# Four graph layers on one core: float32r parts for every source tile of the second layer, evacuation straight out of PSUM, and another split of the first layer's piece buffers

## The chip, the core and the metric

The kernel runs on one core of a Trainium2 chip. A core has a matrix engine (TensorE, in the profile PE, with its weight loads as PEld), VectorE (DVE), ScalarE (ACT), GpSimd (POOL) and SyncE (SP), which here mostly issues transfers. Each engine works through its own list of instructions. The metric is the device time of one execution in microseconds, given as the median of several runs.

## The reference

There are 3327 nodes with 512 features, and one adjacency matrix for all layers. Layers 0 to 2 are graph attention layers with 8, 4 and 8 heads, each behind a layer norm with ReLU and with a residual:

```
h = relu(layernorm(x));  Wh = h @ W, split by heads
e[i, j] = leaky_relu(s1[i] + s2[j], 0.2)     where adj[i, j] > 0, else minus infinity
x = x + elu(softmax_j(e) @ Wh)
```

s1 and s2 are products of Wh with two vectors per head. Layer 1 (the second layer) also sets the diagonal of its mask, and its four heads have 128 features each. Layer 3 averages the neighbours' features, joins them with the node's own, and applies dense weights.

## The kernel before, in words

**The arithmetic.** exp(leaky_relu(s1 + s2)) is exp(s1) exp(s2) where s1 + s2 is positive, and the same with 0.2 times each where it is not. So a head needs no exponent per edge: for each sign there is a 0/1-like matrix (mask and sign, in fp8), multiplied with Wh scaled by exp(s2) or exp(0.2 s2). A column of ones gives the softmax's denominator, so a head of layer 1 has DA = 129 columns. The two results of a target row are scaled by a coefficient of that row (L.c, made by `close_terms`, L561 to L599, from all s1 and s2), added, and divided by the denominator.

**Tiles and groups.** Targets and sources lie in 26 tiles of 128 nodes. Target tiles are taken in chunks of four (the last has two); source tiles come in five groups of 6, 6, 6, 4 and 4 (JG, L67). For each chunk and head, ScalarE or VectorE compares s1 with -s2 for every source tile (L660 to L665; the list GP_ON_DVE names VectorE's tiles), VectorE combines it with the mask (`split`, L668), and TensorE accumulates over the 26 source tiles for two target tiles at a time: one "pass".

**Precision.** The scaled Wh is kept in parts, so that cheap matmuls add up to enough bits. Layers 0 and 2 use three bf16 pieces side by side. In layer 1 the kind of a group (KIND, L49) says how: "b" is three bf16 pieces, 387 columns, multiplied with the fp8 matrix as it is (L756); "s" and "v" are two float32r parts, 258 columns (L753), for which the fp8 matrix must first be cast to float32r by ScalarE ("s", tile ts, three buffers) or by VectorE ("v", tile tv, two buffers), in `real`, L628 to L634. A cast covers one group and the two target tiles of one pass. Before, the kinds are b, s, s, v, v. The parts are made while the previous layer runs (`pieces`, L363; `parts`, L449) and stored to device memory; each head loads them again (L708, tile ab).

**Layer 1, one head.** Two signs times two passes. The matrices of the positive sign are used first; then VectorE flips them in place to the other sign (L788). After each pass VectorE sums the three 129-column pieces of each accumulator into R (L774; the third holds only what group 0 put there). At the head's end R is multiplied by L.c (L796), the signs are added (L798), and the rows are divided into A (L800 to L803). There are four accumulators of one PSUM bank each.

**Layer 0.** Its pieces come in two rings: groups of six tiles in "ab" with 7 buffers, groups of four, once the first pass is over, in "abx" with 3 (`pieces_tile`, L639). All are loaded over SP's queue (L714), where transposing transfers of the adjacency (tile tr, L238, three buffers), mask stores (L252) and the rows of s1 (L676) are issued too.

**Order.** The program's text gives priorities; a planner of the framework then fixes each engine's order when the kernel is built, and an instruction whose inputs and buffer are ready earlier can stand ahead of one written before it. `after` adds orders by hand. Small stages of the next layer (layer norm, transposes, projections) are started once per pass by `hooks.run` (L608, L784).

Of the kernel before, what the change touches and what calls it, by code (L numbers as in the profile page):

```python
# [25 lines left out]
F32 = mybir.dt.float32  # L26
BF16 = mybir.dt.bfloat16
# [10 lines left out]
P = 128  # L38
# [4 lines left out]
S2_MAX = 30.0  # L43
S_CLIP = 40.0

GP_ON_DVE = [(5, 12, 19), tuple(range(18, 26)), (4, 9, 14, 19, 24)]


KIND = "bssvv"  # L49


@with_exitstack
def tile_gnn(ctx: ExitStack, tc: tile.TileContext, x, adj, W0, a01, W1, al, ar, W2, a2,
# [60 lines left out]
    for l in range(3):  # L114
        H, DA, AO, HW = dims(l)
        if l == 1:
            abd.append([dram.tile([H, 2, P, nj, AO], BF16, name=f"ab{l}_{g}") if KIND[g] == "b" else
                        dram.tile([H, 2, P, nj, 2 * DA], F32, name=f"ab{l}_{g}") for g, (_, nj) in enumerate(JG)])
# [92 lines left out]
    def mask_steps(pool, t, g):  # L211


        n = pn(t)
        c, k = where[t]
        j0, nj = JG[g]
        w = min(nj * P, N - j0 * P)
        q = {}

        def load():  # L220
            at = q["at"] = pool.tile([P, JM * P], BF16, name="at", bufs=3)
            if n < P:
                nc.vector.memset(at, 0.0)
            elif w < nj * P:
                nc.vector.memset(at[:, w:nj * P], 0.0)
            ld = nc.gpsimd.dma_start(at[:n, :w], adj[t * P:t * P + n, j0 * P:j0 * P + w])
            after(ld, gone[-1] if gone else stored[NT - 1] if c else relus[-3])

        def turn():
            at = q["at"]  # L230
            if c == 0:
                tp = q["tp"] = ps.tile([P, 8, P], BF16, name="tp", bufs=2)
                for j in range(nj):
                    nc.tensor.transpose(tp[:, j, :], at[:, j * P:(j + 1) * P], identb)
                compare()
            else:
                tp = q["tp"] = mp.tile([P, JM, P], BF16, name="tr", bufs=3)
                tr = nc.sync.dma_start(tp[:, :nj], at[:, :nj * P], transpose=True)  # L238
                after(tr, gone[-1] if gone else stored[NT - 1])

        def compare():
            hooks.done += 1
            tp = q["tp"]
            st = masks0[g][:, k] if c == 0 else pool.tile([P, JM, P], FP8, name="st", bufs=3)[:, :nj]
            cm = nc.vector.tensor_scalar(st, tp[:, :nj], 0.0, 2.0, op0=ALU.is_gt, op1=ALU.mult, saturate=False)
            if gone:
# [116 lines left out]
    def pieces(L, t, AB, pool, first, behind=None):  # L363
# [4 lines left out]

        o, two = (t % 2, 2) if first else (0, 1)
        if o == 0:  # L370
            L.pt = pool.tile([P, H, 2, two, AO] if l == 1 else [P, H, two, HW], BF16, name="pt", bufs=3 if first else 2)
        pt = L.pt
        nc.gpsimd.memset(pt[:, :, :, o, 3 * DA:AO] if l == 1 else
                         pt[:, :, o].rearrange("p h (a w) -> p h a w", a=2)[..., 3 * DA:AO], 1.0)

        def dst(s, a):
            if l == 1:
                return pt[:, :, a, o, s * DA:(s + 1) * DA]
# [14 lines left out]
        if o == two - 1 and l == 1:  # L393
            for a in range(2):
                L.to_store.append((abd[l][g][:, a, :, js, :].rearrange("h p j w -> p h j w"), pt[:, :, a]))
        elif first and o == two - 1:
# [52 lines left out]
    def parts(L, t, AB, pool, first, behind=None):  # L449
# [229 lines left out]
    def attention(L, hooks, open_next, close):  # L679
# [5 lines left out]
        for c, (t0, nt) in enumerate(chunks):  # L685
# [3 lines left out]
            for h in range(H):  # L689
# [10 lines left out]
                for a in range(2 if l == 1 else 1):  # L700
                    row = []
                    for g, (_, nj) in enumerate(JG):
                        if l == 1:
                            tl = mp.tile([P, JM * 2 * DA], F32R, name="ab", bufs=7)
                            two = KIND[g] != "b"
                            w = 2 * DA if two else AO
                            v = (tl if two else tl.bitcast(BF16))[:, :nj * w].rearrange("p (j w) -> p j w", j=nj)
                            ld = nc.sync.dma_start(v.bitcast(F32) if two else v, abd[l][g][h, a])  # L708
# [28 lines left out]
                for a in range(2 if l == 1 else 1):  # L737
# [5 lines left out]
                    for ks, js in passes:  # L743
                        thr = {}
                        for j in js:
                            g, jj = jwhere[j]
                            if l == 1 and KIND[g] != "b" and g not in thr:
                                thr[g] = real(a, g, ks, th)
                            for k in ks:
                                if j == 0:  # L750
                                    acc[k] = accs.tile([P, 512], F32, name="acc")
                                if g in thr:
                                    mm = nc.tensor.matmul(acc[k][:, :2 * DA], thr[g][:, k - ks[0], jj, :], ab[a][g][:, jj, :],  # L753
                                                     start=(j == 0), stop=(j == NT - 1), skip_group_check=True)
                                elif l == 1:
                                    mm = nc.tensor.matmul(acc[k][:, :3 * DA], th[a][g][:, k, jj, :], ab[a][g][:, jj, :3 * DA],  # L756
                                                     start=(j == 0), stop=(j == NT - 1), skip_group_check=True)
                                else:
                                    o = 1 if deg else 0
# [9 lines left out]
                            load_y2(yp, 0, late)  # L769
                        if js[-1] != NT - 1:  # L770
                            continue
                        for k in ks:
                            if l == 1:
                                nc.vector.tensor_reduce(R[:, k, a, :], acc[k][:, :3 * DA].rearrange("p (s d) -> p d s", s=3),  # L774
                                                        AX.X, ALU.add)
# [20 lines left out]
                nc.vector.tensor_mul(Rv, Rv, L.c[:, t0:t0 + nt, :, h:h + 1].to_broadcast([P, nt, 2, DA]))  # L796
                num = R[:, :, 0, :]
                nc.vector.tensor_add(num[:, :nt], Rv[:, :, 0, :], Rv[:, :, 1, :])  # L798
                rc = mp.tile([P, PER, 1], F32, name="rc")
                nc.vector.tensor_scalar(rc[:, :nt], num[:, :nt, DK:DA], S_MIN, None, op0=ALU.max)  # L800
                nc.vector.reciprocal(rc[:, :nt], rc[:, :nt])
# [88 lines left out]
    lay_out(bp, ("ab", JM * 400, BF16, 7))  # L890
    ip = masking.enter_context(tc.tile_pool(name="masks", bufs=1))
    with tc.tile_pool(name="first", bufs=1) as fp:

# [50 lines left out]
    tags = [[A[0], R, tht, ("tr", JM * P, BF16, 3), ("abx", 4 * 400, BF16, 3), gt],  # L944
            [A[1], ("ab", JM * 258, F32R, 7), R, ("ts", 2 * JM * P, F32R, 3), ("tv", 2 * 4 * P, F32R, 2), tht[:3] + (10,)],
            [A[2], ab, ("R", PER * 2 * 65, F32, 1), tht, gt]]
    hooks.masks = in_steps([mask_steps(ip, t, g) for t, g in order[20:]])
    for l in range(3):
# [530 lines left out]
```

## Time and profile before

| what | value |
|---|---|
| median of 3 runs | 3587.35 us (3585.51 to 3601.4) |
| the profiled execution's own time | 3590.36 us |
| its span, first to last instruction | 3588.6 us |
| mean granted TensorE clock | 0.988 |
| busy: PE, PEld, DVE, ACT, POOL | 96%, 87%, 73%, 70%, 18% |
| attention of layer 0 / of layer 1, by the windows view | 202 to 1268 us / 1268 to 2113 us |
| HBM read and written | 663.59 MB, 129.64 MB |

A line of groups names the source line, the engine, the operation, output and input tiles with their shapes and the count; then busy us and the mean ns of one; then the idle time of the engine just ahead of these instructions, and what ended it. A line of the timeline gives start, length, engine, the group and how many were merged; in square brackets stands the idle time ahead of it. The windows view gives each engine's busy time within a stretch. Matmuls overlap, so their pace is read from starts, not from durations.

### The profile page before, as it was taken

The numbers are of one execution on the slowest core, as the hardware profiler recorded it, in microseconds if no ns is written. First come the engines' busy times: TensorE is split into PE (matmuls) and PEld (weight loads), VectorE is DVE, ScalarE is ACT, GpSimd is POOL, SyncE is SP. The second block draws the span as 40 slices with busy tenths as digits, with TensorE's granted clock in tenths as the row PEclk, the third lists the DMA queues.
The fourth block names the chain that finished last, engine by engine and source line by source line (L and its number), as shares of the span: only waits on it lengthen the run. The fifth ranks groups of instructions, "written<-read, shape, count | busy, mean of one in ns | idle before, by whom it ended". The sixth has DMA issues, their size and how long they took to land. (4 is left out here: it accounts for less than half of the span.)

```text
span 3588.6 us, 77637 instructions
## 1 busy us (share of the span) xinstructions
PE 3452.1 (96%) x30751; PEld 3112.2 (87%) x30751; DVE 2622.2 (73%) x5227; ACT 2507.9 (70%) x4113; POOL 632.5 (18%) x858
## 2 busy tenths in 40 slices
PE   7889999999999999999999989999999999999998
PEld 6788999999999878888888869989898989876887
DVE  8777878787887789888888868877676767672221
ACT  5767877877887888888798767766676667572111
POOL 6601222111110211233223230001010101020000
PEclk9999999999999999999999999999999999999999
DMA  7798999999966877777877876655555555576331
GB/s 216 235 239 222 237 249 233 258 236 242 262 217 207 283 277 262 282 258 273 283 256 266 307 280 212 195 174 178 176 195 176 173 178 184 166 264 257 122 99 60
DMA packets 398119, 797.72 MB, mean 222 GB/s; under 512 B 112969, under 2 KB 221844, under 8 KB 397104
## 3 DMA queue, kind: packets, MB, share of 16 engines
q1 hardware_dynamic: 363890, 723.14, 62.5%
q0 software_dynamic: 28128, 62.42, 7.5%
q10 hardware_dynamic: 5726, 7.08, 0.6%
q8 instruction: 245, 4.01, 0.5%
q14 instruction: 130, 1.06, 0.1%
HBM read 663.59 MB, written 129.64 MB: 221 GB/s over the span
## 5 line engine op out<-in xcount | busy, mean ns | idle before, releaser
L664 ACT ACTIVATE gt<-s1b,ks 128x512 fp8e4<-128x512 f32 (+1 forms) x2448 | 1448.0, 677 | 294.3 <-issue 160.1
L760 PE MATMUL acc<-ab,tht 128*128 128x195 bf16 (+1 forms) x9112 | 1558.0, 248 | 11.3 <-DVE tht L668 9.2
L763 PE MATMUL acc<-ab,gt 128*128 128x195 bf16 (+1 forms) x9112 | 1557.1, 248 | 5.7 <-DVE rc L800 3.3
L763 PEld LDWEIGHTS <-gt 128*128 128x128 fp8e4 x10744 | 1055.5, 98 | 64.3 <-issue 41.5
L760 PEld LDWEIGHTS <-tht 128*128 128x128 fp8e4 x10744 | 1055.2, 98 | 35.2 <-DVE tht L668 20.0
L668 DVE TENSOR_TENSOR tht<-gt,m 128x768 uint32<-128x768 uint32 (+3 forms) x557 | 449.8, 808 | 121.8 <-ACT gt L664 120.1
L670 DVE TENSOR_TENSOR gt<-tht,m 128x768 uint32<-128x768 uint32 (+3 forms) x557 | 450.1, 808 | 8.7
L633 ACT CAST ts<-tht 128x1536 fp32r<-128x1536 fp8e4 x208 | 300.0, 1470 | 59.0 <-PE acc L753 54.9
L753 PE MATMUL acc<-ab,ts 128*128 128x258 f32 x2496 | 335.0, 290 | 4.9 <-DMA ab<-ab 2.5
L753 PEld LDWEIGHTS acc<-ab,ts 128*128 128x128 f32 x2496 | 314.6, 191 | 14.4 <-issue 3.3
L661 DVE TENSOR_SCALAR gt<-s1b,ns 128x512 fp8e4<-128x512 f32 (+1 forms) x446 | 217.3, 492 | 133.6 <-PE acc L763 127.9
L1015 PE MATMUL acc<-y,mf 128*128 128x512 f32 x1352 | 309.9, 391 | 2.3 <-DVE mf L1010 2.3
L664 ACT ACTIVATE tht<-s1b,ks 128x512 fp8e4<-128x512 f32 (+1 forms) x504 | 308.3, 680 | 2.9 <-DMA s1b<-s 2.4
L763 PE MATMUL acc<-abx,gt 128*128 128x195 bf16 (+1 forms) x1632 | 288.7, 250 | 20.8 <-DVE rc L800 7.8
L760 PE MATMUL acc<-abx,tht 128*128 128x195 bf16 (+1 forms) x1632 | 289.5, 250 | 19.3 <-DMA abx<-ab 15.5
L1015 PEld LDWEIGHTS acc<-y,mf 128*128 128x128 f32 x1352 | 253.6, 188 | 58.5 <-DVE mf L1010 2.7
L863 POOL TENSOR_TENSOR xt<-xt,e 128x512 f32<-128x512 f32 x72 | 122.1, 1695 | 899.6 <-DVE e L862 586.4
L778 DVE TENSOR_REDUCE R<-acc 128x130 f32<-128x390 f32 x416 | 214.7, 556 | 77.5 <-PE acc L763 76.9
L756 PE MATMUL acc<-ab,tht 128*128 128x387 bf16 x1248 | 226.6, 330 | 9.0 <-DMA ab<-ab 5.4
L1012 ACT CAST mf<-m 128x768 fp32r<-128x768 fp8e4 (+1 forms) x78 | 59.1, 762 | 245.8 <-PE acc L1015 234.0
L753 PE MATMUL acc<-ab,tv 128*128 128x258 f32 x1664 | 219.3, 283 | 2.5 <-DVE tv L633 1.4
L753 PEld LDWEIGHTS acc<-ab,tv 128*128 128x128 f32 x1664 | 207.3, 189 | 4.7 <-DVE tv L633 2.5
(163 smaller groups left out, 3722.6 us busy)
## 6 DMA issues: line engine op xcount, KB each, us to landing
ab<-ab SPq DMA_DIRECT2D x333, 600.0 KB, 5.2
ab<-ab SPq DMA_DIRECT2D x112, 774.0 KB, 6.6
ab<-ab SPq DMA_DIRECT2D x112, 516.0 KB, 5.4
ab<-ab SPq DMA_DIRECT2D x112, 400.0 KB, 3.8
abx<-ab SPq DMA_DIRECT2D x110, 400.0 KB, 6.9
ab<-ab SPq DMA_DIRECT2D x56, 582.0 KB, 7.3
s1b<-s SPq DMA_DIRECT2D x120, 256.0 KB, 6.4
m<-mask SPq DMA_DIRECT2D x69, 384.0 KB, 4.1
```

Source lines behind the costliest of these rows:

```text
L633: (nc.scalar.copy if KIND[g] == "s" else nc.vector.tensor_copy)(t[:, :k1 - k0, :nj], th[a][g][:, k0:k1])
L661: nc.vector.tensor_scalar(gv[:, :, jj, :], s1v, L.ns2[:, j, h:h + 1], 2.0, op0=ALU.is_gt, op1=ALU.mult, saturate=False)
L664: nc.scalar.activation(gv[:, :, jj, :], s1v, AF.Relu, bias=L.ks2[:, j, h:h + 1], scale=BIG, saturate=False)
L668: nc.vector.tensor_tensor(pu, gu, mu, ALU.bitwise_and)
L670: nc.vector.tensor_tensor(gu, pu, mu, ALU.bitwise_xor)
L753: mm = nc.tensor.matmul(acc[k][:, :2 * DA], thr[g][:, k - ks[0], jj, :], ab[a][g][:, jj, :], start=(j == 0), stop=(j == NT - 1), skip_grou ...
L756: mm = nc.tensor.matmul(acc[k][:, :3 * DA], th[a][g][:, k, jj, :], ab[a][g][:, jj, :3 * DA], start=(j == 0), stop=(j == NT - 1), skip_grou ...
L760: nc.tensor.matmul(acc[k][:, :3 * DA + o], th[0][g][:, k, jj, :], ab[0][g][:, jj, :3 * DA + o], start=(j == 0), stop=False, skip_group_che ...
L763: mm = nc.tensor.matmul(acc[k][:, AO:AO + 3 * DA + o], th[1][g][:, k, jj, :], ab[0][g][:, jj, AO:AO + 3 * DA + o], start=False, stop=(j == ...
L778: nc.vector.tensor_reduce(R[:, k], v.rearrange("p a (s d) -> p a d s", s=3), AX.X, ALU.add)
L863: nc.gpsimd.tensor_add(xt, xt, e)
L1015: nc.tensor.matmul(acc[k], mf[:, jj, :], y2[g][:, jj, s, :], start=(j0 + jj == 0 and s == 0), stop=(j0 + jj == NT - 1 and s == 1))
```

## The change

- Group 0 of layer 1 becomes "v": the kinds are v, s, s, v, v. All five groups now use two float32r parts, so every accumulator of layer 1 is 258 columns wide, and the bf16 branches for layer 1 (storing, loading, multiplying) go. tv keeps two buffers, each now for up to six source tiles; tht, the ring of the fp8 matrices of layer 1, goes from 10 to 9 buffers.
- Evacuation in layer 1: instead of one three-piece reduction per accumulator and a scaling and an addition at the head's end, each of the two 129-column halves is multiplied by the row's coefficient straight out of PSUM and added onto R's first plane: four instructions per pass. The coefficients must then exist at the first evacuation, so `close_terms` is called there.
- VectorE's compares of layer 1 go from the eight tiles 18 to 25 to the six tiles 18, 19, 20, 22, 23, 24; 21 and 25 go to ScalarE.
- Layer 0: "ab" 7 to 6 buffers, "abx" 3 to 4, "tr" 3 to 4.

```
-GP_ON_DVE = [(5, 12, 19), tuple(range(18, 26)), (4, 9, 14, 19, 24)]
-KIND = "bssvv"
+GP_ON_DVE = [(5, 12, 19), (18, 19, 20, 22, 23, 24), (4, 9, 14, 19, 24)]
+KIND = "vssvv"
...
-                tp = q["tp"] = mp.tile([P, JM, P], BF16, name="tr", bufs=3)
+                tp = q["tp"] = mp.tile([P, JM, P], BF16, name="tr", bufs=4)
...
-        if l == 1 and KIND[g] != "b":
+        if l == 1:
...
-            tl = mp.tile([P, nj * HW], BF16, name="abx", bufs=3)
+            tl = mp.tile([P, nj * HW], BF16, name="abx", bufs=4)
...
-            tl = pool.tile([P, JM * HW], BF16, name="ab", bufs=7)
+            tl = pool.tile([P, JM * HW], BF16, name="ab", bufs=6 if L.l == 0 else 7)
...
-                        pt = mp.tile([P, PER * JM * P], FP8, name="tht", bufs=10 if l == 1 else 7)
+                        pt = mp.tile([P, PER * JM * P], FP8, name="tht", bufs=9 if l == 1 else 7)
...
-                            if l == 1 and KIND[g] != "b" and g not in thr:
+                            if l == 1 and g not in thr:
                                 thr[g] = real(a, g, ks, th)
...
-                                elif l == 1:
-                                    mm = nc.tensor.matmul(acc[k][:, :3 * DA], th[a][g][:, k, jj, :], ab[a][g][:, jj, :3 * DA],
-                                                     start=(j == 0), stop=(j == NT - 1), skip_group_check=True)
...
+                        if l == 1 and c == 0 and h == 0 and a == 0 and ks[0] == 0:
+                            close_terms(L)
                         for k in ks:
                             if l == 1:
-                                nc.vector.tensor_reduce(R[:, k, a, :], acc[k][:, :3 * DA].rearrange("p (s d) -> p d s", s=3),
-                                                        AX.X, ALU.add)
+                                cf = L.c[:, t0 + k, a, h:h + 1]
+                                for s in range(2):
+                                    v = acc[k][:, s * DA:(s + 1) * DA]
+                                    if a == s == 0:
+                                        nc.vector.tensor_scalar(R[:, k, 0, :], v, cf, None, op0=ALU.mult)
+                                    else:
+                                        nc.vector.scalar_tensor_tensor(R[:, k, 0, :], v, cf, R[:, k, 0, :],
+                                                                       op0=ALU.mult, op1=ALU.add)
...
-                if c == 0 and h == 0:
-                    close_terms(L)
-                Rv = R[:, :nt]
-                nc.vector.tensor_mul(Rv, Rv, L.c[:, t0:t0 + nt, :, h:h + 1].to_broadcast([P, nt, 2, DA]))
                 num = R[:, :, 0, :]
-                nc.vector.tensor_add(num[:, :nt], Rv[:, :, 0, :], Rv[:, :, 1, :])
+                if l != 1:
+                    if c == 0 and h == 0:
+                        close_terms(L)
+                    Rv = R[:, :nt]
+                    nc.vector.tensor_mul(Rv, Rv, L.c[:, t0:t0 + nt, :, h:h + 1].to_broadcast([P, nt, 2, DA]))
+                    nc.vector.tensor_add(num[:, :nt], Rv[:, :, 0, :], Rv[:, :, 1, :])
...
-            [A[1], ("ab", JM * 258, F32R, 7), R, ("ts", 2 * JM * P, F32R, 3), ("tv", 2 * 4 * P, F32R, 2), tht[:3] + (10,)],
+            [A[1], ("ab", JM * 258, F32R, 7), R, ("ts", 2 * JM * P, F32R, 3), ("tv", 2 * JM * P, F32R, 2), tht[:3] + (9,)],
```

More of the change, by code (lines that the diff above doesn't have):

```diff
@@ L116, in tile_gnn @@
         if l == 1:
-            abd.append([dram.tile([H, 2, P, nj, AO], BF16, name=f"ab{l}_{g}") if KIND[g] == "b" else
-                        dram.tile([H, 2, P, nj, 2 * DA], F32, name=f"ab{l}_{g}") for g, (_, nj) in enumerate(JG)])
+            abd.append([dram.tile([H, 2, P, nj, 2 * DA], F32, name=f"ab{l}_{g}") for g, (_, nj) in enumerate(JG)])
         else:
@@ L370, in pieces @@
         if o == 0:
-            L.pt = pool.tile([P, H, 2, two, AO] if l == 1 else [P, H, two, HW], BF16, name="pt", bufs=3 if first else 2)
+            L.pt = pool.tile([P, H, two, HW], BF16, name="pt", bufs=3 if first else 2)
         pt = L.pt
-        nc.gpsimd.memset(pt[:, :, :, o, 3 * DA:AO] if l == 1 else
-                         pt[:, :, o].rearrange("p h (a w) -> p h a w", a=2)[..., 3 * DA:AO], 1.0)
+        nc.gpsimd.memset(pt[:, :, o].rearrange("p h (a w) -> p h a w", a=2)[..., 3 * DA:AO], 1.0)
         def dst(s, a):
-            if l == 1:
-                return pt[:, :, a, o, s * DA:(s + 1) * DA]
             return pt[:, :, o, a * AO + s * DA:a * AO + (s + 1) * DA]
@@ L392, in pieces @@
         js = slice(jj + 1 - two, jj + 1)
[L393 to L396, printed above, removed]
+        if first and o == two - 1:
             if g not in ahead:
@@ L704, in attention @@
                             tl = mp.tile([P, JM * 2 * DA], F32R, name="ab", bufs=7)
[L705 to L708, printed above, removed]
+                            v = tl[:, :nj * 2 * DA].rearrange("p (j w) -> p j w", j=nj)
+                            ld = nc.sync.dma_start(v.bitcast(F32), abd[l][g][h, a])
                         else:
@@ L751, in attention @@
                                     acc[k] = accs.tile([P, 512], F32, name="acc")
-                                if g in thr:
+                                if l == 1:
                                     mm = nc.tensor.matmul(acc[k][:, :2 * DA], thr[g][:, k - ks[0], jj, :], ab[a][g][:, jj, :],
-                                                     start=(j == 0), stop=(j == NT - 1), skip_group_check=True)
-                                elif l == 1:
-                                    mm = nc.tensor.matmul(acc[k][:, :3 * DA], th[a][g][:, k, jj, :], ab[a][g][:, jj, :3 * DA],
                                                      start=(j == 0), stop=(j == NT - 1), skip_group_check=True)
@@ L889, in tile_gnn @@
     bp = masking.enter_context(tc.tile_pool(name="pieces", bufs=1))
-    lay_out(bp, ("ab", JM * 400, BF16, 7))
+    lay_out(bp, ("ab", JM * 400, BF16, 6))
     ip = masking.enter_context(tc.tile_pool(name="masks", bufs=1))
@@ L943, in tile_gnn @@
     ab, gt, tht = ("ab", JM * 400, BF16, 7), ("gt", PER * JM * P, FP8, 7), ("tht", PER * JM * P, FP8, 7)
-    tags = [[A[0], R, tht, ("tr", JM * P, BF16, 3), ("abx", 4 * 400, BF16, 3), gt],
-            [A[1], ("ab", JM * 258, F32R, 7), R, ("ts", 2 * JM * P, F32R, 3), ("tv", 2 * 4 * P, F32R, 2), tht[:3] + (10,)],
+    tags = [[A[0], R, tht, ("tr", JM * P, BF16, 4), ("abx", 4 * 400, BF16, 4), gt],
+            [A[1], ("ab", JM * 258, F32R, 7), R, ("ts", 2 * JM * P, F32R, 3), ("tv", 2 * JM * P, F32R, 2), tht[:3] + (9,)],
             [A[2], ab, ("R", PER * 2 * 65, F32, 1), tht, gt]]
```

## The prediction

> **What bounds the kernel now.** I read the page's slices first (TensorE at nine tenths nearly everywhere, granted clock 0.988), then cut the span by layer with the windows view, then took groups, timeline and waits of the two layers touched. The page's chain of waits covers only the last layer (TensorE, L1015), so it says nothing on this change. Columns of the windows view: length, busy us of PE, PEld, DVE, ACT, POOL, clock, DMA share, GB/s.
>
> ```profile
> 1268.00:2113.00 845.00, 825.94 (x5946) 719.55 (x5946) 730.59 (x1376) 706.35 (x969) 211.87 (x231) 0.99 0.78 279
> 202.00:1268.00 1066.00, 1015.18 (x11060) 984.69 (x11057) 844.39 (x1785) 825.50 (x1459) 182.48 (x274) 0.99 0.89 240
> ...
> 1368.00:1468.00 100.00, 100.00 (x749) 88.52 (x747) 91.72 (x173) 88.94 (x116) 21.72 (x22) 1.00 0.76 272
> ```
>
> First row: attention of layer 1 (the "second layer"), TensorE 98%, but VectorE already 86% and ScalarE 84%. Second: attention of layer 0, TensorE 95%, DMA 89%. In the second layer's best 100 us VectorE reaches 92% while TensorE never waits. So the second layer is TensorE's, with little room beneath.
>
> One pass of the second layer in the timeline (start, length from first start to last end, engine, group):
>
> ```profile
> 1512.97 2.15 PE L756 MATMUL acc<-ab,tht 128*128 128x387 bf16 x12
> 1514.82 3.18 PE L753 MATMUL acc<-ab,ts 128*128 128x258 f32 x24
> 1517.83 2.08 PE L753 MATMUL acc<-ab,tv 128*128 128x258 f32 x16
> 1519.75 2.15 PE L756 MATMUL acc<-ab,tht 128*128 128x387 bf16 x12
> ```
>
> A pass takes 1519.75 - 1512.97 = 6.78 us. The 16 tv matmuls pass in 1.92 us, 0.120 each; at that pace 40 float32r matmuls take 4.80, which leaves 1.98 for 12 bf16 ones, 0.165 each. (Durations in the groups, 283 and 330 ns, overlap.)
>
> What VectorE does around a pass's end:
>
> ```profile
> 1386.11 0.70 DVE L633 CAST tv<-tht 128x1024 fp32r<-128x1024 fp8e4 x1 [0.62 <-PE acc L753]
> ...
> 1386.87 2.15 PE L756 MATMUL acc<-ab,tht 128*128 128x387 bf16 x12
> ...
> 1386.95 1.03 DVE L774 TENSOR_REDUCE R<-acc 128x129 f32<-128x387 f32 x2
> ```
>
> The cast for the next pass stands ahead of this pass's reductions, though the program writes it after them: the order comes from the planner, and the cast starts as soon as its buffer is free. Group 0 needs no cast today, so TensorE enters the next pass without VectorE.
>
> Groups of the second layer (count, busy us, mean ns):
>
> ```profile
> L633 DVE CAST tv<-tht 128x1024 fp32r<-128x1024 fp8e4 x208 | 146.1, 703 | 58.1 <-PE acc L753 58.1
> L774 DVE TENSOR_REDUCE R<-acc 128x129 f32<-128x387 f32 x207 | 105.8, 554 | 9.5 <-PE acc L753 8.7
> ...
> L796 DVE TENSOR_TENSOR R<-R,cpm 128x1032 f32<-128x1032 f32 x24 | 33.1, 1380 | 0.0
> ...
> L798 DVE TENSOR_TENSOR R<-R 128x516 f32<-128x516 f32 x24 | 17.4, 726 | 0.0
> ```
>
> In the first layer, what TensorE waited for ahead of the four-tile pieces:
>
> ```profile
>   DMA abx<-ab: 15.5, 7
>   DVE rc L800: 7.8, 7
>   DVE rc L801: 5.9, 3
>   DVE gt L670: 5.9, 4
>   DVE tht L668: 3.6, 4
> ```
>
> With two small ones that is 39.8 us, once per head at the same place. A matmul reading pieces does not need rc, so those rows are probably the late transfer too.
>
> [...]
>
> **The change, part by part.**
>
> *TensorE.* The second layer has 13 pairs of target tiles x 4 heads x 2 signs = 104 passes (208 reductions / 2). Each has 12 bf16 matmuls turned float32r: 12 x 0.045 = 0.54 us, pass 6.24. Sum 104 x 0.54 = 56 us saved, if nothing takes it.
>
> *The added cast.* L1010 casts 768 in 559 and 512 in 427 ns; L633 casts 1024 in 703. The line through them gives about 0.95 us for 1536 elements (bounds 0.90 to 1.05); 104 of them, 99 us of VectorE. Its place matters more. tv keeps two buffers, but now serves three groups a pass, in order 0, 3, 4. The next group 0 takes the buffer of this group 3, free when TensorE ends it; TensorE then has only group 4 left, 8 x 0.12 = 0.96 us. If group 4 starts at t, the last group 3 matmul ends at t + 0.16, a cast starts 0.10 later (as at 1511.90), ends at t + 1.21, and TensorE could go on at about t + 1.26, where it wants t + 0.96. So 0.30 us per pass is lost even with VectorE idle; with one instruction of 0.4 to 1.0 us in progress, some 0.35 more. I take 0.50: 52 us. Projections of the next layer (24 tiles, 3.56 us each by the timeline) and transposes can fill part; they exist in about half of the passes, so I take a third off: 35 us.
>
> *Evacuation.* Out: 106 us of reductions, 36 of L796 (its 516 form included), 20 of L798. In: 416 instructions of 129 elements out of PSUM. No row shows one. L1024 (512, PSUM and SBUF) takes 751 ns[...]; L427 (tiny, PSUM) takes 0.16[...]. 104 x 0.29 + 312 x 0.34 = 136 us; bounds 100 (0.24 each, well overlapped) to 150. Accumulators have four buffers, two per pass, so their later release (1.3 us instead of 1.0) lies under the next pass.
>
> *Compares.* Two of eight tiles per head go from VectorE (L661, 104 us in all, so 26) to ScalarE (710 ns, 38 us). ScalarE loses about 8 us with the old pieces of six tiles: 706 + 30 = 736, still under the stage's length.
>
> *VectorE's sum.* 731 - 106 - 36 - 20 - 26 + 99 + 136 = 778; about 200 more instructions, each starting some 0.06 us before its predecessor ends, take 12 off: 766. Storing six tiles in the new form costs and saves about 8 each.
>
> *Moves and buffers.* closing the terms stands before the first evacuation, not at the head's end: its VectorE, TensorE, ScalarE chain now holds the first accumulators; once, 3 us (0 to 8). tht falls from 10 to 9, so the next head's group 4 (about 2 us on VectorE) waits until the last pass of this head; it is needed 5 us into the next: nothing if VectorE keeps up, and crowding where it doesn't. Group 0's loads grow from 582 to 774 KB x 56 = 10.7 MB; at 279 GB/s for 0.78 of the engines that is about 30 us of engine time, share 0.78 to about 0.83, hidden by the 7-deep ring.
>
> *First layer.* Large pieces 7 to 6 is exactly two heads of three, and a slot's refill has more than one head (17.5 us) to land. Small ones 3 to 4: today group 4 of the next head waits on SP's queue until the last pass of this head is nearly over, about 8.8 us before its use, with 6.9 us median and 11.6 maximum to land, and SP's later issues stand behind it. With four it gets a whole head more. Of 39.8 us I take 24, because DMA share there is 0.96 over 200 to 1000 us and the bytes are unchanged; bounds 0 and 40.
>
> *Sum.* TensorE's account of the second layer: 845 - 56 + 35 + 3 = 827. VectorE's: 766 at the best density seen, 0.917, is 836. I take the middle, 831, so -14; first layer -24; together -38. Against the profiled execution (span 3588.6, time 3590.36) that is 3552; the median shown is 3587.35, so 3549.
>
> **Rivals.** (a) *VectorE hides it all*: boundaries filled, first layer gains its 38: -56 - 38 + 3 = -91, 3496. For: 114 us idle on VectorE today. Against: 0.30 us per pass is structural. (b) *VectorE becomes the bound*: density 0.885 gives 867, +22 - 24 = -2, 3585. For: ordered waits stall it (58 us), and now both engines wait for each other each pass. (c) *Slower*: the planner puts the group 0 cast behind the four evacuations, which wait for the pass's last matmul. TensorE then waits 0.2 + 4 x 0.3 + 0.95 + 0.05 = 2.4 us per pass; 60 to 100% unfilled is 150 to 250, less 56 and 24: about +110, 3700. It decides from a stall of (56 + 24 + 18)/104 = 0.94 us per pass. Against: casts are placed ahead today. (d) *No first-layer gain*, DMA being full: -14, 3573.
>
> **Numbers.** Forecast 0.40 (own range 3535 to 3570), (a) 0.14, (b) 0.24, (c) 0.14, (d) 0.08. Range 3490 to 3610: nearly all of forecast, (b) and (d), most of (a), not (c). A measurement here tells 0.5% (18 us) from no change. Faster (under 3569): 0.38 + 0.14 + 0.05 + 0.02 = 0.59; same: 0.02 + 0.13 + 0.06 = 0.21; slower: 0.06 + 0.14 = 0.20.
>
> **What would show it.** Right: passes of 6.2 us of matmuls plus 0.3 to 0.6 of TensorE waiting on the group 0 cast; the second layer 820 to 840 with VectorE above 90%; waits ahead of abx under 20 us; evacuations near 0.3 us. Wrong: TensorE waits above 0.9 us per pass, casts behind evacuations in VectorE's order, or abx waits unchanged.

## The result, and the profile after

The changed kernel takes 3628.05 us (median of five runs, 3621.0 to 3635.67) against 3595.8 us for the kernel before, in runs beside it: a ratio of 1.0084 (95% interval 1.0066 to 1.0102). It is slower by 0.84%, about 30 us, where 1.1% faster was forecast, and it lies above the range. The forecast of 3549 us started from 3587.35, the median of three runs of the kernel before; beside the changed kernel that kernel took 3595.8, so some 8 us of the distance are the starting point's. The profiled execution took 3628.05 us, with a span of 3626.3 us and a mean granted clock of 0.978 (0.988 before).

I cut both profiles at the same events: the first and the last matmul on the small pieces (tile abx), which are the beginning and the end of the first layer, and the last matmul on tv, which ends the second. Windows view of the kernel after, the first layer and then the second:

```profile
206.60:1267.80 1061.20, 1005.63 (x11000) 980.92 (x10999) 832.69 (x1773) 808.98 (x1428) 156.78 (x243) 0.98 0.91 240
1267.80:2147.70 879.90, 812.89 (x5999) 770.64 (x5997) 774.18 (x1590) 749.78 (x1041) 266.94 (x245) 0.97 0.80 283
```

The same two stretches of the kernel before:

```profile
202.10:1249.40 1047.30, 998.54 (x11002) 975.21 (x11000) 837.33 (x1767) 814.30 (x1440) 173.35 (x259) 0.99 0.90 241
1249.40:2111.60 862.20, 841.27 (x5997) 727.97 (x5995) 736.43 (x1390) 716.95 (x985) 221.00 (x246) 0.99 0.77 276
```

In the second layer TensorE's busy time fell by 28 us (841.27 to 812.89), half of the 56 worked out. Its idle time, length less busy, rose by 46 (20.9 to 67.0). VectorE and ScalarE have 38 and 33 us more to do. The layer became 17.7 us longer. Its granted clock fell from 0.99 to 0.97: the traces give the clock as full or half, and TensorE was busy at half clock for 11.2 us of the second layer before and for 41.7 after (last section). The first layer reads 13.9 us longer in this profile; the first experiment shows that its new buffers alone do not do that.

A pass of the second layer after, in the timeline:

```profile
1535.62 2.08 PE L743 MATMUL acc<-ab,tv 128*128 128x258 f32 x16
...
1536.78 0.96 DVE L625 CAST tv<-tht 128x1536 fp32r<-128x1536 fp8e4 x1 [0.56 <-PE acc L743]
...
1537.66 1.12 DVE L770 SCALAR_TENSOR_TENSOR R<-acc,cpm,R 128x129 f32<-128x129 f32 x4
1537.80 1.50 PEld L743 LDWEIGHTS acc<-ab,tv 128*128 128x128 f32 x12 [0.27 <-DVE tv L625]
1537.80 1.71 PE L743 MATMUL acc<-ab,tv 128*128 128x258 f32 x12
...
1539.34 3.04 PE L743 MATMUL acc<-ab,ts 128*128 128x258 f32 x24
...
1544.40 1.50 PEld L743 LDWEIGHTS acc<-ab,tv 128*128 128x128 f32 x12 [0.31 <-DVE tv L625]
```

VectorE waits for a buffer (0.56 us), casts group 0 (0.96), and TensorE's weight load waits for it (0.27) even here, where VectorE is on time. The cast still stands ahead of the evacuations, here and in nearly every pass. From one group 0 to the next it is 1544.40 - 1537.80 = 6.60 us, against 6.78 before and 52 x 0.12 = 6.24 of matmuls: 0.36 lost at this boundary.

Groups of the second layer after, by form, which answer to the casts, reductions, scalings and additions shown of before:

```profile
L625 DVE CAST tv<-tht 128x1024 fp32r<-128x1024 fp8e4 x208 | 152.9, 749 | 8.6 <-PE acc L743 8.3
L625 DVE CAST tv<-tht 128x1536 fp32r<-128x1536 fp8e4 x104 | 102.3, 984 | 40.6 <-PE acc L743 39.6
L770 DVE SCALAR_TENSOR_TENSOR R<-acc,cpm,R 128x129 f32<-128x129 f32 x309 | 89.1, 343 | 5.1 <-PE acc L743 5.1
L768 DVE TENSOR_SCALAR R<-acc,cpm 128x129 f32<-128x129 f32 x104 | 31.4, 344 | 0.8 <-ACT cpm L591 0.7
```

And the waits of TensorE in the second layer after (total us, times, longest):

```profile
PE acc L743 <- DVE tv L625: 34.7, 34, 4.4
PE mm L399 <- ACT hT L140: 9.8, 2, 9.1
PE acc L743 <- ACT ts L625: 6.6, 3, 2.4
PE mm L399 <- DVE AB L436: 5.4, 3, 2.6
PE acc L743 <- issue: 4.3, 1, 4.3
```

Before, the tv row was 1.4 us, 3 times. Single waits of 4.4 us are far longer than the 0.36 of a boundary: there the cast comes late. The trace tells why. 19 of the tv waits last at least 0.5 us, 30.5 us together. Ahead of 15 of them VectorE was at work for at least 92% of the 6 us before its cast. Ahead of the other four, the two of 4.4 us among them, it had itself stood waiting for ScalarE (ahead of the wait that ends at 1696.06 us, for 2.4 us at a combination with the mask, L660, that needs ScalarE's compare).

In the first layer after, what TensorE waited for ahead of the small pieces:

```profile
  DVE rc L797: 16.9, 10
  DVE tht L660: 16.2, 10
  DVE gt L662: 6.2, 4
  DVE rc L798: 5.2, 3
  DMA mask<-st: 3.4, 1
```

The row "DMA abx<-ab" of before, 15.5 us, is gone, as the fourth buffer promised. The sum did not fall: 47.9 us against 39.8.

### The profile page after: what moved, and what is told of

Same layout as the page of the kernel before. It is cut to its first block, busy times and chain, and to the rows that moved or that the text cites. A ratio compares the mean times of both kernels' runs of the same rounds, so it can differ in the third digit from the quotient of the medians.

```text
span 3626.3 us, 77977 instructions
## 1 busy us (share of the span) xinstructions
PE 3432.4 (95%) x30751; PEld 3161.4 (87%) x30751; DVE 2654.1 (73%) x5433; ACT 2536.4 (70%) x4157; POOL 650.6 (18%) x840
## 5 line engine op out<-in xcount | busy, mean ns | idle before, releaser
L660 DVE TENSOR_TENSOR tht<-gt,m 128x768 uint32<-128x768 uint32 (+3 forms) x557 | 445.7, 800 | 120.4 <-ACT gt L656 118.6
L743 PE MATMUL acc<-ab,tv 128*128 128x258 f32 x2912 | 406.7, 291 | 43.3 <-DVE tv L625 34.7
L743 PEld LDWEIGHTS acc<-ab,tv 128*128 128x128 f32 x2912 | 373.3, 193 | 59.0 <-DVE tv L625 47.4
L656 ACT ACTIVATE tht<-s1b,ks 128x512 fp8e4<-128x512 f32 (+1 forms) x560 | 344.6, 681 | 1.9 <-DMA s1b<-s 1.6
L743 PE MATMUL acc<-ab,ts 128*128 128x258 f32 x2496 | 323.3, 286 | 6.9 <-ACT ts L625 6.6
L653 DVE TENSOR_SCALAR gt<-s1b,ns 128x512 fp8e4<-128x512 f32 (+1 forms) x446 | 218.4, 495 | 133.1 <-PE acc L750 132.7
L625 DVE CAST tv<-tht 128x1024 fp32r<-128x1024 fp8e4 (+1 forms) x312 | 255.1, 828 | 49.2 <-PE acc L743 47.9
```

The costliest lines, as they stand in the source:

```text
L625: (nc.scalar.copy if KIND[g] == "s" else nc.vector.tensor_copy)(t[:, :k1 - k0, :nj], th[a][g][:, k0:k1])
L653: nc.vector.tensor_scalar(gv[:, :, jj, :], s1v, L.ns2[:, j, h:h + 1], 2.0, op0=ALU.is_gt, op1=ALU.mult, saturate=False)
L656: nc.scalar.activation(gv[:, :, jj, :], s1v, AF.Relu, bias=L.ks2[:, j, h:h + 1], scale=BIG, saturate=False)
L660: nc.vector.tensor_tensor(pu, gu, mu, ALU.bitwise_and)
```

## The experiments

The causes held against each other were the shared ring tv, the load and lateness of VectorE, the new evacuation with its earlier closing terms, the compares that moved to ScalarE, and the first layer's buffers. Each ratio is against the kernel before, with its 95% interval; the length of a layer is that of one profile. Lines that only lay out the memory of the tiles are left out of the edits shown.

**The first layer's part alone.** The kernel before with

```
-tp = q["tp"] = mp.tile([P, JM, P], BF16, name="tr", bufs=3)
+tp = q["tp"] = mp.tile([P, JM, P], BF16, name="tr", bufs=4)
...
-tl = mp.tile([P, nj * HW], BF16, name="abx", bufs=3)
+tl = mp.tile([P, nj * HW], BF16, name="abx", bufs=4)
...
-tl = pool.tile([P, JM * HW], BF16, name="ab", bufs=7)
+tl = pool.tile([P, JM * HW], BF16, name="ab", bufs=6 if L.l == 0 else 7)
```

> The kernel before with only the three first-layer buffer counts of the change (large pieces 6, small 4, transposes 4). Theory A (these buffers change the order on SP's queue and cost the 18 us that the first layer lost): first layer ends near 1265 us instead of 1249, ratio 1.003 to 1.006. Theory B (the first layer's loss comes along with the second layer's edits, which the planner weighs in the same list): first layer ends at 1250 or earlier, ratio 0.99 to 1.001. As I forecast before the change ran: first layer 24 us shorter, ratio 0.993.

Ratio 1.0005 (0.9994 to 1.0016), first layer 1047.6 us, 1047.3 before. The split of the buffers is worth nothing that shows, neither a gain nor a loss.

**The second layer's part alone.** The kernel after with the minus lines of the diff above in place of its plus lines.

> The changed kernel with the first layer's buffers as before (7, 3, 3): the second layer's edits alone. Theory A: first layer ends near 1250 again, and only the second layer's loss of about 17 us remains: ratio 1.003 to 1.006. Theory B: the first layer still ends near 1267, ratio 1.008.

Ratio 1.0085 (1.0058 to 1.0112), the second layer 883.3 us, the first 1051.4. The whole loss comes from the second layer's edits, but not all of it lies in the second layer: 21 of some 30 us do (see the end of the next section).

**A ring of its own for group 0.** The kernel after with

```
-t = mp.tile([P, 2, nj, P], F32R, name="ts" if KIND[g] == "s" else "tv", bufs=3 if KIND[g] == "s" else 2)
+t = mp.tile([P, 2, nj, P], F32R, name="ts" if KIND[g] == "s" else "tv" if g else "tw",
+            bufs=3 if KIND[g] == "s" else 2 if g else 1)
```

> The changed kernel, but group 0's cast has a buffer of its own (one for six tiles) and groups 3 and 4 keep two of four tiles. Theory C (the second layer lost at the pass boundaries, since group 0's cast had to wait for group 3's matmuls): waits of TensorE and of its weight loads on tv casts fall from 82 us to under 25, second layer 830 us or less instead of 856, ratio 0.995 to 1.001 against before. Theory D (VectorE's load of 764 us is what bounds, the ring only names the place): waits move to other VectorE results, second layer stays at 850 to 860, ratio 1.007 to 1.009.

Ratio 1.0049 (1.0032 to 1.0066), between the two forecasts. TensorE's waits in the second layer of this run:

```profile
PE acc L743 <- DVE tw L625: 23.5, 17, 4.1
PE acc L743 <- ACT ts L625: 11.2, 5, 3.5
PE mm L399 <- ACT hT L140: 9.4, 2, 8.7
PE acc L743 <- issue: 8.9, 2, 4.7
PE mm L399 <- DVE AB L436: 5.8, 4, 2.6
PE acc L743 <- DVE tv L625: 0.9, 2, 0.7
```

The layer takes 863.5 us, 16.4 less than after; 13.9 of it are busy time (812.89 to 798.99). An estimated 6 us of these are fewer matmuls at half clock (TensorE was busy at half clock for 30.5 us, 41.7 after). The rest can be the short gap at each boundary, which stood in the "busy" of after: the matmul ends are drawn past the next start, so the first 0.16 us of a gap (0.28 long, 0.12 from start to start) doesn't show as idle. The idle time stays, 64.5 us. In 23.5 of them TensorE waits for group 0's cast, which now has its buffer most of a pass early and is late all the same, in 17 waits of up to 4.1 us. Ahead of 15 of the 17 VectorE was at work for at least 97% of the 6 us before the cast; in nine (9.2 us) more than 2 us of these were flips (L784).

**The old evacuation.** The kernel after with one reduction per accumulator, of two pieces, the scaling and addition at the head's end, and the terms closed there:

```
-for s in range(2):
-    v = acc[k][:, s * DA:(s + 1) * DA]
...
+nc.vector.tensor_reduce(R[:, k, a, :], acc[k][:, :2 * DA].rearrange("p (s d) -> p d s", s=2), AX.X, ALU.add)
```

> The changed kernel with the evacuation undone: one reduction over the two parts per accumulator, scaling and addition at the head's end, terms closed at the first head's end. Per head of four tiles VectorE gets 16 reductions of about 0.42 us, one scaling of 1.2 to 1.4 and one addition of 0.7 instead of 32 instructions of 0.34: 8.7 us against 11.0 by durations, 5 to 7 after overlaps. Theory D (VectorE's load bounds): second layer 20 us or more shorter, ratio 1.001 to 1.004. Theory C (boundaries by the ring): within 8 us of the changed kernel, ratio 1.006 to 1.010, apart from some 5 us at the first head where the terms are closed later.

Ratio 1.0081 (1.0054 to 1.0107), the second layer 887.0 us. VectorE works 787.75 us, 13.6 more than after, where less was expected. A reduction took 0.416 us here, as estimated (0.42). The form of the evacuation makes no difference that shows in the time.

**Less for VectorE.** The kernel after without the flip; the negative sign's matrix is not made, and the positive one is used twice:

```
-nc.vector.tensor_tensor(pu, pu, mu, ALU.bitwise_xor)
+pass
```

> The changed kernel without the in-place flips of the second layer (140 instructions, about 109 us of VectorE); its result leaves out the negative sign's matrices, which are then those of the positive sign again. The shared tv ring stays. Theory C (ring): gap of about 0.3 us per pass stays (the matmuls' end to the cast's end is unchanged), second layer 850 us or more, ratio above 1.001. Theory D (VectorE's load): the ring's residue is small and the waits shrink with the load, second layer 825 to 840, ratio 0.993 to 0.998. Both true: about 840, ratio 0.998.

Ratio 0.9997 (0.9987 to 1.0007). VectorE falls to 683.60 us, the layer to 852.4: 27.5 us come back though TensorE's matmuls are the same. The layer is as long as expected of the ring (850 or more), the ratio lower than expected of it (above 1.001). Less load is not all that this edit brings: it also clears blocks of flips from ahead of casts, and the second sign's casts no longer wait for a flip. No run separates these.

**Both.** Without the flips as well as with group 0's own ring.

> The same without flips, and group 0's cast in a buffer of its own. TensorE then has neither the ring nor VectorE's load (about 670 of 860 us) against it: if these two are the whole cause, the 56 us saved on matmuls come through: second layer 805 to 815 us against 862 before, ratio 0.985 to 0.989. If something else holds TensorE (ScalarE's casts, the clock, transfers), it stays above 835, ratio 0.994 or more.

Ratio 0.9932 (0.9907 to 0.9958). Windows view of this run's second layer:

```profile
1263.00:2091.10 828.10, 792.92 (x5997) 762.86 (x5995) 680.04 (x1450) 741.38 (x1041) 219.16 (x245) 0.98 0.83 300
```

TensorE is idle for 35.2 us and busy for 792.9. The two causes together give 51.8 us, 8 more than 16.4 + 27.5. The layer is still 13 us or more above what I expected of it. TensorE was busy at half clock for 29.7 us here, 11.2 before, which is worth an estimated 9 us; waits for ScalarE's casts (8.0 us) are among the rest.

**Group 0's cast on GpSimd**, in its own buffer with the tiles as in the run with the own ring.

```
-(nc.scalar.copy if KIND[g] == "s" else nc.vector.tensor_copy)(t[:, :k1 - k0, :nj], th[a][g][:, k0:k1])
+(nc.scalar.copy if KIND[g] == "s" else nc.vector.tensor_copy if g else nc.gpsimd.tensor_copy)(
+    t[:, :k1 - k0, :nj], th[a][g][:, k0:k1])
```

> The changed kernel with group 0's cast on GpSimd and in a buffer of its own: the whole computation, VectorE 102 us lighter, GpSimd 104 casts more. By the 1.4 to 1.7 us that GpSimd takes for 512 fp32 elements of two inputs, 1536 elements of one input take 2 to 4.5 us, 210 to 470 us on top of the 264 us it works in this layer. Theory D: second layer 825 to 840, ratio 0.993 to 0.999 against before, unless a cast of more than some 5 us doesn't fit between the free buffer (after group 0's matmuls) and the next pass. If GpSimd slows VectorE while both work, VectorE's mean durations rise and the gain is lost: 850 or more.

Ratio 1.0056 (1.0039 to 1.0073), second layer 866.7 us: the forecast for a GpSimd that slows VectorE. The costliest group of GpSimd in this run:

```profile
L625 POOL CAST tw<-tht 128x1536 fp32r<-128x1536 fp8e4 x104 | 192.9, 1855 | 224.6 <-PE acc L743 205.2 <-DVE tht L660 11.9 <-DVE tht L784 6.9
```

A cast takes GpSimd 1.86 us. VectorE's casts of the four-tile groups in the same run:

```profile
L625 DVE CAST tv<-tht 128x1024 fp32r<-128x1024 fp8e4 x208 | 172.3, 830 | 30.3 <-PE acc L743 30.1
```

103 us of casts left VectorE, yet its busy time fell only from 777.55 us (own ring) to 765.92: its own casts went from 704 to 830 ns each, its compares (L653) from 607 to 656, its six-tile flips (L784) from 950 to 1056; its evacuations out of PSUM (L770) stayed at 340 to 342. So in the run in which GpSimd casts, VectorE's casts, compares and flips took 8 to 18% longer than with the own ring; why they did, no run here shows.

**The compares back on VectorE**, with group 0's own ring.

```
-GP_ON_DVE = [(5, 12, 19), (18, 19, 20, 22, 23, 24), (4, 9, 14, 19, 24)]
+GP_ON_DVE = [(5, 12, 19), tuple(range(18, 26)), (4, 9, 14, 19, 24)]
```

> The changed kernel with group 0's cast in a buffer of its own and the compares as before (eight tiles per head on VectorE, so VectorE about 26 us more, ScalarE about 38 us less). Against the own-ring kernel (1.0049, second layer 863): if VectorE is what is short, 8 to 25 us more, ratio 1.007 to 1.012; if ScalarE is, 10 to 30 us less, ratio 0.997 to 1.002.

Ratio 1.0032 (1.0018 to 1.0046), between the two forecasts and no worse than with the own ring alone, though VectorE has 16 us more to do (793.80). ScalarE has 29 less (712.88). So it isn't VectorE's sum alone that counts; what ScalarE's lighter load gives back was not measured apart.

**No cast of group 0.** Its matmuls read group 1's cast tile, so group 0's sums are computed from group 1's matrix.

```
+if l == 1 and g not in thr and g == 0:
+    thr[0] = thr[1] = real(a, 1, ks, th)
```

> The changed kernel, but group 0's matmuls read the cast tile of group 1, so the cast of group 0 is left out (the sums of group 0 are computed from group 1's matrix); everything else, TensorE's 40 + 12 float32r matmuls per pass included, stays. If the loss is the cast alone (its 102 us of VectorE and its place in the shared ring), VectorE falls to about 675 us in the second layer, as in the run with its own buffer and no flips, and the layer takes 815 to 830 us: ratio 0.990 to 0.995. If float32r itself is what takes the gain back (granted clock, more loads of pieces), the layer stays at 845 us or more, ratio above 0.997, with waits at tv no longer in the list.

Ratio 0.9965 (0.9954 to 0.9977), between the two forecasts. Windows view of its second layer:

```profile
1256.70:2093.70 837.00, 793.11 (x5998) 760.98 (x5996) 683.22 (x1487) 741.58 (x1041) 209.88 (x246) 0.98 0.83 298
```

The layer is 42.9 us shorter than after and 25.2 shorter than before. 16.6 of its 43.9 idle us are waits for ScalarE's cast, which this edit needs earlier in the pass. By the ratio the gain is 0.35%, about half of those 25 us. So float32r for group 0 does gain when its cast costs nothing, and the cast takes more than that.

**Group 0's conversion alone.** The kernel before with group 0 in float32r, its own buffer and nine of tht; evacuation, compares and the first layer as before.

> The kernel before with only group 0 in float32r, cast by VectorE into a buffer of its own, and tht 9: the evacuation, the compares and the first layer's buffers are those of before. If the parts simply add as measured so far (own ring +0.49%, old compares -0.17%, old evacuation and the first layer's buffers nothing), ratio 1.001 to 1.005 and a second layer of 858 to 870 us. If the old evacuation's later release and VectorE's 14 us more load tell once the ring is out of the way, above 1.006. A version better than before would need under 0.998, which no theory of mine gives.

Ratio 1.0037 (1.0025 to 1.0049), second layer 866.4 us: as expected. None of the mixtures of these edits that were tried and compute the whole result was faster than before.

**What holds up the first layer.** With four small buffers no load is late, yet TensorE waits. The timeline of the run with the first layer's part alone, around its longest wait there:

```profile
395.54 0.43 DVE L245 TENSOR_SCALAR st<-tr 128x512 fp8e4<-128x512 bf16 x1 [4.38 <-DMA tr<-at]
395.88 0.42 DVE L798 TENSOR_TENSOR R<-R 128x260 f32<-128x260 f32 x1
...
396.22 0.69 DVE L670 TENSOR_TENSOR gt<-tht,m 128x512 uint32<-128x512 uint32 x1
...
396.82 0.16 DVE L800 TENSOR_SCALAR rc<-R 128x4 f32<-128x4 f32 x1
...
397.05 0.24 PE L763 MATMUL acc<-abx,gt 128*128 128x195 bf16 x1 [4.33 <-DVE rc L800]
```

VectorE stands 4.38 us at the conversion of the next chunk's mask (L245), whose transposing transfer has not landed. The matrix of group 4 (L670) is queued behind it, and TensorE goes on 0.14 us after that is done. "rc", the instruction in progress at that moment, is named in its place. VectorE's waits for that transfer in the first layer of the same run:

```profile
DVE st L245 <- DMA tr<-at: 66.4, 25, 6.1
...
DVE d L250 <- DMA tr<-at: 31.8, 12, 6.7
```

98 us, and 93.6 in the kernel before. Of TensorE's 27 waits of at least 0.5 us for attention in this layer, 21 (34 of 41 us) end within 4 us after the end of such a stall; these stretches of 4 us make up 15% of the layer. To try it, the kernel with the first layer's buffers gets one empty step between the transfer and the conversion:

```
-return (load, turn) if c == 0 else (load, turn, compare)
+return (load, turn) if c == 0 else (load, turn, lambda: None, compare)
```

> The kernel before with the first layer's new buffers (as in the run with those alone), and the mask's conversion on VectorE written one step of the hooks later, so that a transposing transfer has a whole pass more to land. If TensorE's waits ahead of the four-tile pieces are VectorE standing at that conversion (98 us of waits for the transfer there, 21 of TensorE's 27 long waits in the first layer come within 4 us after one), VectorE's waits for it fall below 50 us, TensorE's waits in the first layer from 46 to 20 to 30 us, the layer from 1047 to 1025 to 1035 us: ratio 0.993 to 0.997. If the transfers themselves are the limit (DMA share 0.90), something else is late in the same places and the layer stays at 1043 to 1051 us: ratio 0.999 to 1.001.

Ratio 0.9912 (0.9895 to 0.9928), better than forecast. VectorE's waits for the transfer in the first layer:

```profile
DVE d L250 <- DMA tr<-at: 40.8, 14, 6.7
...
DVE st L245 <- DMA tr<-at: 4.4, 1, 4.4
```

The waits at L245 are all but gone; those at the diagonal's instruction (L250) stay. The first layer of this run in the windows view:

```profile
194.30:1213.50 1019.20, 995.41 (x11012) 976.06 (x11010) 840.66 (x1769) 818.70 (x1448) 173.57 (x259) 0.99 0.93 249
```

28 us less than with the first layer's part alone, TensorE's idle time down from 46.8 to 23.8 us, and the DMA share up from 0.89 to 0.93: the transfers were not the limit, the place of the conversion in VectorE's order was. The mask's store moves with the conversion, but SP's waits at that store did not shrink much (119.5 to 110.7 us), so it is not SP's queue that was freed. Another 12 us are gained ahead of this layer, which starts at 194.3 us in place of 206.3. And on the kernel before with nothing else changed:

> The kernel before with nothing but the later conversion: the first layer's buffers stay seven, three and three. If the conversion's place was the whole matter, the ratio is that of the run with the new buffers as well, 0.990 to 0.993. If the new split of the buffers is worth something once the conversion is out of the way, the 15.5 us of waits for loads into the three small buffers stay, and the ratio is 0.994 to 0.998.

Ratio 0.9906 (0.9888 to 0.9923), median 3561.01 against 3592.01 us, first layer 1023.6 us: the conversion's place is the whole gain, and again the buffers add nothing that shows, though 13.1 us of waits for loads into the three small buffers are still there. This one-line edit, in place of the change, beats both kernels. What it does together with the change was not tried.

## Why the prediction was wrong

**TensorE's work: right; its clock was left out.** 56 us off 841 is 785. With the boundary out of the way the runs show 793 (no cast; own ring and no flips) to 799 (own ring). The pace is as forecast: the 24 matmuls of ts in the pass above take 0.12 each. Of the 8 to 14 us that are missing, an estimated 6 to 10 are matmuls at half clock: 23.2 us (no cast), 29.7 (own ring and no flips) and 30.5 (own ring) of TensorE's busy time, 11.2 before. That term was never in the sum.

**The added cast: place right, price partly.** 0.95 us forecast, 0.984 measured; the line through the three casts that the prediction names gives 0.98, so the shortfall is in its reading. A loss at each boundary of 0.30 or more was argued from the two buffers, and 0.36 is there in a pass with VectorE on time. "I take a third off: 35 us" was too much for the boundary alone: taking the ring away gives back 16.4 us, or 24.3 without the flips (852.4 to 828.1).

**Evacuation: nearly right; compares: too large.** 0.29 and 0.34 us were forecast, 0.344 and 0.343 measured. The two forecasts, and the 136 us made of them, were the author's estimates: the two durations named beside them (751 ns for 512 elements, 0.16 us for a tiny instruction) do not give them. The compares were to move 26 us off VectorE and 38 onto ScalarE; the run with the old ones has 16 and 29. Neither part moves the time beyond the intervals.

**VectorE's sum: right, and wrongly used.** 766 us were forecast for the stretch that was 1268 to 2113 us before, from the layer's first matmul of attention on; that stretch is 1293 to 2149 us after, 856 us long, and VectorE works 764 in it. (Instructions that follow one another on VectorE overlap by 0.085 us at the median in that stretch of before, where the prediction has 0.06: 200 of them take 17 off and not 12.) The step that failed is "TensorE's account ... VectorE's ... I take the middle, 831". It treats each engine as a queue of its own, of which the longer account sets the time. But they hand each other something several times a pass: VectorE waits for tv buffers from TensorE (47.9 us in the layer after), and TensorE for casts from VectorE (34.7). Here, at 88% busy, VectorE's lateness comes on top of TensorE's account; it isn't hidden in it. And a wait was priced at its own length, though a long one can also be followed by half clock (6.83 us of it at the wait of 2.87 in the last section). The runs size both together: 27.5 us come back when 91 us are taken from VectorE (774.18 to 683.60), and 35.4 with group 0's own ring (863.5 to 828.1). With that term, measured afterwards, added to the account in place of a middle, the layer's sign is the measured one: 827 + 27 is 854, against 845 before and 856 measured. "The second layer's best 100 us", VectorE at 92% without a wait of TensorE, was a stretch that the kernel can have, not one that it can keep.

**First layer: wrong by the whole term.** -24 was forecast, nothing came. "A matmul reading pieces does not need rc, so those rows are probably the late transfer too" is the step that failed; and with 27 waits in 56 heads the stall is not in every head, as the prediction has it. The first half is right; the rows named "rc" are VectorE's group 4 matrix, late behind a mask conversion that waits for another transfer. Even the 15.5 us that the trace did put down to the loads were no gain: with those loads on time, the next thing was late at the same place. What would be late next was not asked.

**The rivals.** Of the mechanisms, (b), VectorE as the bound, and (d), no first-layer gain, both came true, and together: (b) without its 24 us is 867 - 845 = +22, 3609, or 3618 from the 3595.8 us measured beside the change; the run took 3628. The two were given chances as alternatives, though nothing excludes both at once, and no case held that sum. In the layer itself (b) was too high, 867 against 856; what it lacked lies outside the layer. (c) is refuted by the order in the timeline: casts ahead of evacuations, 1536.78 and 1537.66. Of the signs listed, evacuations near 0.3 us and passes with 0.3 to 0.6 of waiting are there; the second layer at 820 to 840, VectorE above 90% and waits ahead of abx under 20 are not. Of the signs of being wrong, abx waits that do not fall came true.

In sum: with a free cast the change would make the second layer 25 us shorter, as far as the run without the cast tells; the cast in its place costs 43, and the difference is the 17.7 us that the layer lost. That is not the whole loss. Between the two profiles another 13.9 us lie in the first layer and 4.5 before it, and this is not the scatter of one profile: in each of the ten runs with group 0 in float32r the time, by its ratio, grew by 4 to 16 us more, or fell by that much less, than the second layer did (own ring: the layer 1.3 us longer, the time 0.49%, 17.6 us). In the first layer TensorE was busy at half clock for 38.5 us after and 23.5 before, an estimated 7.5 of the 13.9 us. The four profiles with the old evacuation and the old place of the mask's conversion have first layers of 1043 to 1048 us, the eight with the new evacuation 1050 to 1061. Why edits of the second layer are felt in the first, no run shows.

## What to carry to other kernels

When two engines hand each other tiles several times per pass and both are nearly full (here 92% and 88%), add the second engine's lateness to the first one's account (here some 27 us of an 880 us layer); don't take the longer of the two. Before giving a wait to a buffer, look at what the producing engine did in the 5 us before it: an engine standing at an instruction that has nothing to do with the waiting one (here VectorE, 4.38 us at L245) is found in its own timeline, and not under the name that the wait bears. Moving such an instruction one step later (here a conversion that follows a transfer) can be worth more than a precision or buffer change; here it made the kernel 0.94% faster, where the change made it 0.84% slower.

## What the runs showed that I had not expected

A wait of TensorE can make the matmuls after it slower. Two starts on group 0's tile, timeline of the run with its own ring:

```profile
1351.35 2.92 PE L743 MATMUL acc<-ab,tw 128*128 128x258 f32 x12 [2.87 <-DVE tw L625]
1354.07 2.79 PE L743 MATMUL acc<-ab,ts 128*128 128x258 f32 x12
...
1545.51 1.72 PE L743 MATMUL acc<-ab,tw 128*128 128x258 f32 x12 [1.20 <-DVE tw L625]
```

The windows view of the stretch around the first (the clock is the third number from the end):

```profile
1350.67:1357.50 6.83, 6.15 (x28) 6.18 (x29) 6.41 (x13) 5.56 (x10) 0.00 (x0) 0.50 1.01 415
```

After 1.20 us of waiting, 12 matmuls take 1.72 us; after 2.87 they take 2.92, and the 12 behind them 2.79. The clock stands at half for 6.83 us, of which TensorE works 6.15; in the 3.41 us ahead of it TensorE had been idle for 2.19. At 0.24 us a matmul in place of 0.12, half of that is lost: this wait of 2.87 us cost about 6, by that estimate.

How much idle time it takes can be read from the fourteen traces of this case. In them the clock is full or half, never between, and it changes on a grid of 3.41 us that keeps its place through the run, to within 0.01 us. I counted the steps of that grid in the first two layers that ended at full clock, 7542 in all. Each of the 178 steps in which TensorE was idle for 2.0 us or more was followed by half clock; of the 60 steps with 1.7 to 2.0 us idle, 21 were, and of the 7304 with less, one. So in these traces it was enough that TensorE idled for somewhat more than half of a step, 2.0 us of the 3.41. The half clock goes with the idling and not with float32r: in the last layer of both kernels 1352 float32r matmuls (tile mf, 310 us) run without any half clock.

In the whole run TensorE was busy at half clock for 75.6 us before and 125.4 after. Half of the difference, an estimated 25 us of TensorE's time where the two profiles are 38 us apart, is the price that the added waits have beside their own length. Where the record gives the mean clock of a run, it was 0.984 to 0.989 for the kernel before, 0.977 to 0.980 for the kernel after, and 0.989 to 0.991 for the two with the later conversion.
